# Attention block in float32: operand sums moved between GpSimd and VectorE, stores and loads reordered, fixed operand slots

## Chip, cores and metric

One core of one Trainium2 chip. The time is the device time of one execution in microseconds (us). All arithmetic is float32.

## The reference

x is 4 batches of 512 rows by 1024. The block computes `x + s * g`, with both branches fed by the layer-normed rows `xn`:

```
q = rmsnorm(xn @ Wq.T) * q_norm_w      32 heads of 128, k and v 8 heads (groups g of 4 query heads)
scores = q @ k.T / sqrt(128) + alibi bias, causal;  attn = softmax(scores)
s = concat_heads(attn @ v) @ Wo.T
g = silu(xn @ W.T + bias + lora(xn))   8 adapters of rank 16, weighted
```

## The kernel before, in words

Every large product is done as Strassen-Winograd: seven products of half-size blocks instead of eight, with block sums ahead of them and behind. The seven have the names `A11B11, A12B21, S2T2, S1T1, S3T3, A22T4, S4B22` (L36); S1 to S4 are sums of quadrants of the left operand, T1 to T4 of the right one.

**Front.** The rows are layer-normed, transposed, and the seven left operands of each half batch are written to the DRAM tile `xs`. The left half of the gate product (`f0`) is computed here, its result stored in the DRAM tile `pre`.

**Attention** runs over 32 *units*: a group g (8) and in it a batch b (4). I number them 0 to 31, n = 4 g + b. The order of SyncE (all loads: `sync_dma`), VectorE, ScalarE and TensorE is the order in the program (`in_order`, L69 to L94); GpSimd's is the scheduler's. The loop over units is L685 to L724:

- `fill` is a generator of the 14 projection products (q, k, v) of the *next* unit; each `steps(fill, 1)` issues one. Its left operands stream in from `xs` (`a<-xs`, up to 6 ahead, L433).
- *Lead phase*: eight such steps. Between them SyncE issues 16 `qkT<-flat` transfers of this unit (`turn_qk`, L478) and 16 `pt<-turned` transfers of the unit before (`spread`, L574), three pt per step. Both rearrange data across partitions.
- `attend` (L503): scores, the bias and row minimum on VectorE, exp on ScalarE, and `vector.transpose` of the probabilities into the one buffer `turned`. A new unit may write `turned` only when all 16 pt transfers of the last have read it. PSUM for scores has 3 buffers, `pr` has 6.
- `values` (L587) of the unit before runs late in `attend`: 10 products `ov<-pt,v`, copied by ScalarE to `oh`. Then GpSimd makes the left-operand sums S1 to S4 of the output product, four `tensor_tensor` on `oh` (L607 to L610), and stores all seven left operands in the DRAM tile `lo` of batch b (L611, 1792 KB).
- In odd units `out_sums` (L635) loads two rows of blocks of `wo` (1024 KB), makes the right-operand sums T1 to T4 on GpSimd (L641 to L644) and stores them in the DRAM tile `wt` (L645, 1024 KB).
- The weights of the next group are loaded in units with b = 0 and b = 2, and summed on GpSimd (`right_sums`, L198 to L201).

The last unit has the right half of the gate product (`f1`) for batch 0 as its fill; batch 1 goes beside its `spread`; then come its `values`, then batches 2 and 3 (L725 to L735).

**Output stage** (L738 on): s @ Wo.T as Strassen on two levels. 2 batch pairs times 7 outer products make 14 *items*, each of 7 inner products (`products`, L859) of 16 matmuls of 128x128x256. Inner operands: four quadrants left (`l`, from `lo`, 1 MB each) and right (`r`, from `wo` or `wt`, 1 MB each), four *head sums* (S, 128x2048, VectorE) and four *column sums* (T, 128x2048, GpSimd). `prepare` (L758) makes an item's operands while the item before is multiplied: a `yield` stands after each inner product. It takes tiles from two rings of 9 buffers. One head sum is issued at the fourth of its steps, the other three together at the sixth (L803 to L805), three column sums at the seventh (L807 to L809). Bank `u` takes the products 1, 3 and 5; VectorE saves it (`k`, L888) between these. In 8 of 14 items the finished quadrant is multiplied with the gate, `silu(pre + bias)`, added to x and stored (`gate`, `finish`, L835 to L855). The operands of the first item are loaded after the front pools are closed (L945).

Of the kernel before, what the change touches and what calls it, by code (L numbers as in the profile page):

```python
# [50 lines left out]
def kernel(  # L51
# [87 lines left out]


# [64 lines left out]
    with ExitStack() as front:  # L205
# [207 lines left out]
        with ExitStack() as mid:  # L413
            apool = mid.enter_context(tc.tile_pool(name="left", bufs=6))
            unit = mid.enter_context(tc.tile_pool(name="unit", bufs=2))
            work = mid.enter_context(tc.tile_pool(name="work", bufs=2))
            keep = mid.enter_context(tc.tile_pool(name="keep", bufs=1))
            ps_ov = mid.enter_context(tc.tile_pool(name="ps_ov", bufs=2, space=PSUM))
# [12 lines left out]
            loaded, later = {}, []  # L431
# [13 lines left out]
            def project_qkv(u, b, right, held):  # L445
                flat = unit.tile([P, 4, NT, G + 1, 32], F32, tag="flat", name=f"flat_{u}", bufs=1)
# [31 lines left out]
            def turn_qk(u, held):  # L478
                flat = held.pop("flat")
                qkT = unit.tile([P, 4, NT, G + 1, 32], F32, tag="qkT", name=f"qkT_{u}", bufs=1)  # L480
                for a in range(4):
                    for r in range(4):
                        sync_dma(
                            out=qkT[32 * a : 32 * a + 32, r].rearrange("p t h e -> p (t h e)"),
                            in_=flat[32 * r : 32 * r + 32, a].rearrange("p t h e -> p (t h e)"),
                        )
                        if (4 * a + r) % 5 == 4:
                            yield
                held["qkT"] = qkT

            def scale_k(u, held):
                qkT = held["qkT"]
                kT = unit.tile([P, NT, 4, 32], F32, tag="kT", name=f"kT_{u}", bufs=1)
                vector.tensor_scalar(
                    kT,
                    qkT[:, :, :, 0, :].rearrange("p r t e -> p t r e"),
                    w_sb,
                    None,
                    ALU.mult,
                )  # L500
                held["kT"] = kT
# [72 lines left out]
            def spread(u, held):  # L574
                pt = unit.tile([P, G, npairs, P], F32, tag="pt", name=f"pt_{u}", bufs=1)
                src = turned.rearrange("p m n t e -> p m (n t e)")
                for h in range(G):
                    for m in range(4):
# [4 lines left out]
                        if (4 * h + m) % 3 == 2:  # L583
                            yield
                held["pt"] = pt

            def values(u, g, b, held):  # L587
                pt, v = held["pt"], held["v"]
                oh = unit.tile([P, NP, 2, 2, P], F32, tag="oh", name=f"oh_{u}", bufs=1)
                for i in range(NT):  # L590
# [16 lines left out]
                nc.gpsimd.tensor_tensor(oh[:, S1T1], a21, a22, ALU.add)  # L607
                nc.gpsimd.tensor_tensor(oh[:, S3T3], a11, a21, ALU.subtract)
                nc.gpsimd.tensor_tensor(oh[:, S2T2], oh[:, S1T1], a11, ALU.subtract)
                nc.gpsimd.tensor_tensor(oh[:, S4B22], a12, oh[:, S2T2], ALU.subtract)  # L610
                nc.gpsimd.dma_start(  # L611
                    out=lo[b][:, g], in_=oh.rearrange("p i k m q -> p i (k m) q")
# [22 lines left out]
            def out_sums(g, k):  # L635
# [5 lines left out]
                nc.gpsimd.tensor_tensor(b11, b12, b11, ALU.subtract)  # L641
                nc.gpsimd.tensor_tensor(b12, b22, b12, ALU.subtract)
                nc.gpsimd.tensor_tensor(b22, b22, b11, ALU.subtract)
                nc.gpsimd.tensor_tensor(b21, b22, b21, ALU.subtract)  # L644
                nc.gpsimd.dma_start(  # L645
                    out=wt[k][:, :, :, g, :].rearrange("p i n c -> p (i n) c"),
                    in_=w.rearrange("p k n (m c) -> p (k n m) c", m=2),
# [8 lines left out]
            def last_gate(b):  # L656
                if b == 0:
                    rights["f1"] = weight_operands(raw.pop(HKV), 4, "f1")
                yield from project(
                    f"f1_{b}", b, 4, stream(f"f1_{b}", b), rights["f1"], store_gate(b, 1)  # L660
                )

            def bias_of(g):
                bias = unit.tile([P, SPAN], F32, tag="bias", name=f"bias_{g}", bufs=1)
# [20 lines left out]
            for n, (g, b) in enumerate(units):  # L685
# [3 lines left out]
                fill = start_project(*units[n + 1]) if n + 1 < len(units) else last_gate(0)  # L689
                done = 0  # L690
                for _ in turn_qk(u, held[g, b]):
                    steps(fill, 1)
                    done += 1
                rest = iter(())
                if before is not None:
                    for _ in spread(f"{before[0]}_{before[1]}", held[before]):
                        steps(fill, 1)
                        done += 1
                        if done == LEAD - 2:
                            scale_k(u, held[g, b])  # L700
                    rest = values(f"{before[0]}_{before[1]}", *before, held.pop(before))
                else:
                    steps(fill, LEAD - 2 - done)
                    scale_k(u, held[g, b])
# [5 lines left out]
                for k, _ in enumerate(attend(u, g, b, held[g, b], bias)):  # L710
                    steps(fill, (1, 1, 1, 1, 1, 2, 0, 0)[k])
# [14 lines left out]
            fill = last_gate(1)  # L726
            for _ in spread(u, held[before]):
                steps(fill, 1)
            for _ in fill:
                pass  # L730
            for _ in values(u, *before, held.pop(before)):
                pass
            for b in range(2, B):
                for _ in last_gate(b):
                    pass  # L735


    with ExitStack() as back:  # L738
# [3 lines left out]
        right = back.enter_context(tc.tile_pool(name="right", bufs=9))  # L742
        left = back.enter_context(tc.tile_pool(name="heads", bufs=9))
# [3 lines left out]
        sync_dma(out=bias_bc, in_=bf.to_broadcast([P, D]))  # L747

        QC = D // 4
        quads = (11, 12, 21, 22)  # L750
        part = lambda q: ((q // 10 - 1), (q % 10 - 1))
        wo_of = {A11B11: (0, 0), A12B21: (1, 0), S4B22: (1, 1)}
        wt_of = {S1T1: 0, S3T3: 1, A22T4: 2, S2T2: 3}

        for n in range(6):
            right.tile([P, HKV, QC], F32, tag="r", name=f"rest_{n}")

        def prepare(bp, i, ops):  # L758
            name = f"{bp}_{i}"

            def rt(n):
                return right.tile([P, HKV, QC], F32, tag="r", name=f"r{n}_{name}")

            def lt(n):
                return left.tile([P, 2, HKV, P], F32, tag="l", name=f"l{n}_{name}")

            def load_right(q):
                w = rt(q)
                k, n = part(q)
                if i in wo_of:  # L770
                    kh, nh = wo_of[i]
                    c0 = 512 * nh + QC * n
                    sync_dma(
                        out=w,
                        in_=wo[:, :, 2 * kh + k, c0 : c0 + QC].rearrange("g p c -> p g c"),
                    )
                else:
                    sync_dma(out=w, in_=wt[k][:, wt_of[i], n])
                return w

            def load_left(q):
                a = lt(q)
                m, k = part(q)
                for b in range(2):
                    sync_dma(out=a[:, b], in_=lo[2 * bp + b][:, :, i, 2 * k + m, :])
                return a

            b12, a21 = load_right(12), load_left(21)
            b11, a11 = load_right(11), load_left(11)
            b21, a12 = load_right(21), load_left(12)  # L790
            yield
            t2, s2 = rt(2), lt(2)
            yield
            t1, s1 = rt(1), lt(1)
            nc.gpsimd.tensor_tensor(t1, b12, b11, ALU.subtract)
            yield
            t3, s3 = rt(3), lt(3)
            vector.tensor_tensor(s3, a11, a21, ALU.subtract)
            yield
            t4, a22 = rt(4), load_left(22)  # L800
            yield
            b22, s4 = load_right(22), lt(4)
            vector.tensor_tensor(s1, a21, a22, ALU.add)  # L803
            vector.tensor_tensor(s2, s1, a11, ALU.subtract)
            vector.tensor_tensor(s4, a12, s2, ALU.subtract)  # L805
            yield
            nc.gpsimd.tensor_tensor(t2, b22, t1, ALU.subtract)  # L807
            nc.gpsimd.tensor_tensor(t3, b22, b12, ALU.subtract)
            nc.gpsimd.tensor_tensor(t4, t2, b21, ALU.subtract)  # L809
            ops.update(  # L810
                {
                    A11B11: (a11, b11),
                    A12B21: (a12, b21),
                    S2T2: (s2, t2),
                    S1T1: (s1, t1),
                    S3T3: (s3, t3),
                    A22T4: (a22, t4),
                    S4B22: (s4, b22),
                }
            )  # L820
# [38 lines left out]
        def products(bp, i, ops):  # L859
# [12 lines left out]
            def product(acc, p, start):  # L872
                a, w = ops[p]
# [69 lines left out]
        items = [(bp, i) for bp in range(2) for i in range(NP)]  # L943
        ops = {}
        for _ in prepare(*items[0], ops):  # L945
            pass
        for n, (bp, i) in enumerate(items):
            after = {}
            ahead = prepare(*items[n + 1], after) if n + 1 < len(items) else iter(())
            for _ in products(bp, i, ops):  # L950
                next(ahead, None)
            ops = after
# [40 lines left out]
```

## Time and profile before

| | |
|---|---|
| median of 3 runs (lowest, highest) | 2836.09 us (2822.3, 2838.67) |
| profiled execution: time, span | 2833.2 us, 2831.3 us |
| TensorE busy, VectorE, ScalarE, GpSimd | 93%, 52%, 28%, 35% of the span |
| granted TensorE clock, mean | 0.98 |
| front, until the first qkT transfer | 0 to 229 us |
| attention, 31 units with the next unit beside them | 229 to 1920 us |
| last unit and right gate half | 1920 to 2072 us |
| output stage | 2076 to 2831 us |

In the lines of the timeline the first two numbers are start and length in us, then engine, line, operation, `out<-in`, shape and how many were merged; `[3.0 <-X]` says that the engine stood idle 3.0 us before and that X ended it. `SPq` are DMA issues of SyncE: the length is that of the issue, not of the transfer. Line 92, 77 and 87 are the recording helpers for matmul, for VectorE and ScalarE, and for SyncE's transfers, so the tiles tell the instructions apart. A suffix `_p` is the q, k, v projection, `_f` the gate, `_o` the output stage.

### The profile page before, as it was taken

The numbers are of one execution on the slowest core, as the hardware profiler recorded it, in microseconds if no ns is written. First come the engines' busy times: TensorE is split into PE (matmuls) and PEld (weight loads), VectorE is DVE, ScalarE is ACT, GpSimd is POOL, SyncE is SP. The second block draws the span as 40 slices with busy tenths as digits, with TensorE's granted clock in tenths as the row PEclk, the third lists the DMA queues.
The fourth block names the chain that finished last, engine by engine and source line by source line (L and its number), as shares of the span: only waits on it lengthen the run. The fifth ranks groups of instructions, "written<-read, shape, count | busy, mean of one in ns | idle before, by whom it ended". The sixth has DMA issues, their size and how long they took to land.

```text
span 2831.3 us, 29439 instructions
## 1 busy us (share of the span) xinstructions
PE 2645.1 (93%) x9448; PEld 1777.3 (63%) x9448; DVE 1461.3 (52%) x3211; ACT 793.0 (28%) x2112; POOL 1002.3 (35%) x740
## 2 busy tenths in 40 slices
PE   6898999999999999999999999998869999999998
PEld 4664555555555555555555555556658887888877
DVE  5315455455545545645454555454035547755465
ACT  1113344334434434434343444344000000000000
POOL 5331232332332332242143143233133543535433
PEclk9999999999999999999999999999989999999999
DMA  5633776777678678678767876776786656675652
GB/s 220 248 130 112 210 215 178 213 206 220 194 208 238 176 216 218 192 205 212 207 172 222 208 209 189 218 217 182 227 248 197 209 163 197 199 213 191 200 180 73
DMA packets 344537, 561.43 MB, mean 198 GB/s; under 512 B 32320, under 2 KB 222784, under 8 KB 334784
## 3 DMA queue, kind: packets, MB, share of 16 engines
q1 hardware_dynamic: 328464, 450.48, 57.1%
q0 software_dynamic: 14080, 92.28, 8.8%
q10 hardware_dynamic: 1840, 16.78, 1.5%
q8 instruction: 77, 1.26, 0.2%
q14 instruction: 76, 0.62, 0.1%
HBM read 324.54 MB, written 109.05 MB: 153 GB/s over the span
## 4 chain that ended last, share of the span: by engine, by line
PE 61%; DMA 14%; SPq 9%; issue 6%; DVE 6%; POOL 3%; ACT 1%; ACTq 0%; POOLq 0%; DVEq 0%
PE c_p L92 15%; PE u_p L92 10%; SPq L87 9%; PE c_o L92 9%; PE ov L92 8%; PE u_o L92 8%; DMA pt<-turned 7%; PE sc L92 6%; DMA a<-xs 3%; PE c_f L92 3%; PE u_f L92 2%; DVE l L77 1%; DMA row<-in_x_dram 1%; DVE ms L77 1%; ACT pr L77 1%
## 5 line engine op out<-in xcount | busy, mean ns | idle before, releaser
L92 PE MATMUL c_o<-r,l 128*128 128x256 f32 x1792 | 393.6, 379 | 0.0
L92 PEld LDWEIGHTS c_o<-r,l 128*128 128x128 f32 x1792 | 340.5, 190 | 46.3
L92 PE MATMUL c_p<-t_q,a 128*128 128x384 f32 x1024 | 357.8, 493 | 9.7 <-DMA a<-xs 8.6
L92 PE MATMUL u_o<-r,l 128*128 128x256 f32 x1344 | 314.3, 394 | 56.2 <-DVE k L77 33.9
L77 DVE TENSOR_TENSOR c_p<-c_p,k_p 128x384 f32<-128x384 f32 x192 | 107.1, 558 | 484.3 <-ACT k_p L77 274.0
L92 PE MATMUL u_p<-t_q,a 128*128 128x384 f32 x1024 | 353.1, 488 | 3.2 <-DMA a<-xs 2.9
L77 ACT ACTIVATE pr<-sc,low 128x128 f32<-128x128 f32 (+12 forms) x512 | 248.5, 488 | 383.4 <-DVE low L77 219.4
L92 PE MATMUL c_p<-b,a 128*128 128x384 f32 x1024 | 351.7, 486 | 0.5 <-DMA a<-xs 0.5
L92 PE MATMUL sc<-kT,qkT 128*128 128x128 f32 (+12 forms) x1024 | 300.0, 410 | 46.3 <-ACT pr L77 46.1
L92 PEld LDWEIGHTS u_o<-r,l 128*128 128x128 f32 x1344 | 266.5, 199 | 98.4 <-issue 54.2
L92 PE MATMUL ov<-pt,v 128*128 128x512 f32 x640 | 291.4, 594 | 0.0
L92 PEld LDWEIGHTS sc<-kT,qkT 128*128 128x128 f32 x1024 | 178.6, 191 | 174.0 <-ACT pr L77 75.8
L92 PEld LDWEIGHTS c_p<-t_q,a 128*128 128x128 f32 x1024 | 195.3, 193 | 140.3 <-issue 11.1
L451 POOL COPY v<-c_p 128x128 f32<-128x128 f32 x128 | 37.8, 295 | 685.9 <-DVE c_p L77 685.9
L92 PEld LDWEIGHTS c_p<-b,a 128*128 128x128 f32 x1024 | 192.2, 190 | 128.9 <-PE sc L92 0.8
L77 DVE STREAM_TRANSPOSE turned<-pr 128x128 f32<-128x128 f32 (+6 forms) x800 | 214.3, 332 | 113.8 <-DMA a<-xs 35.3
L92 PEld LDWEIGHTS u_p<-t_q,a 128*128 128x128 f32 x1024 | 191.4, 190 | 128.0 <-DMA a<-xs 7.1
L77 DVE CUSTOM_DVE_ANT_0 sc<-sc,bias 128x128 f32<-128x128 f32 (+12 forms) x512 | 223.7, 466 | 59.3 <-PE sc L92 56.8
L77 ACT ACTIVATE pr<-pr,rden 128x128 f32<-128x128 f32 (+12 forms) x512 | 230.3, 522 | 83.6 <-DVE rden L77 83.3
L77 DVE TENSOR_TENSOR l<-l,l 128x2048 f32<-128x2048 f32 x56 | 211.0, 3768 | 35.9 <-DMA l<-lo 31.9
L92 PEld LDWEIGHTS ov<-pt,v 128*128 128x128 f32 x640 | 121.5, 191 | 145.4 <-issue 126.4
L462 POOL TENSOR_TENSOR inv<-ms,neg_half 128x5 f32<-128x5 f32 x128 | 149.9, 1181 | 176.4 <-DVE ms L77 176.4
(112 smaller groups left out, 2798.4 us busy)
## 6 DMA issues: line engine op xcount, KB each, us to landing
a<-xs SPq DMA_DIRECT2D x448, 256.0 KB, 5.3
pt<-turned SPq DMA_DIRECT2D x512, 160.0 KB, 5.1
lo<-oh POOLq DMA_DIRECT2D x32, 1792.0 KB, 8.2
l<-lo SPq DMA_DIRECT2D x112, 512.0 KB, 7.6
qkT<-flat SPq DMA_DIRECT2D x512, 80.0 KB, 2.6
r<-wt SPq DMA_DIRECT2D x32, 1024.0 KB, 6.7
r<-in_wo_dram SPq DMA_DIRECT2D x24, 1024.0 KB, 6.3
b<-in_wq_dram SPq DMA_DIRECT2D x32, 512.0 KB, 7.5
```

The lines of the kernel that those rows point to most:

```text
L77: ins = getattr(self.engine, op)(*args, **kw)
L87: ins = nc.sync.dma_start(**kw)
L92: ins = nc.tensor.matmul(*args, **kw)
L451: nc.gpsimd.tensor_copy(v[:, t, :], c[:, G + 1, :])
L462: nc.gpsimd.tensor_tensor(inv, ms, neg_half, ALU.pow)
```

## The change

1. `values` no longer sums on GpSimd. The four S sums on `oh` become VectorE instructions, put as closures into the list `spare`; the last also issues the `lo` store. `out_sums` does the same with T and the `wt` store. In the lead phase, `lead()` issues one product of `fill` and then pops one closure of `spare`, first in first out: eight per unit.
2. The last unit has the gate products of batches 0 and 1 as its fill, two per step of `attend`. Its `spread` is cut into 16 steps of one transfer, beside the 28 gate products of batches 2 and 3; its `values` come after all of them.
3. Tiles that end with the last `attend` (`flat`, `qkT`, `kT`, `bias`, `pr`, `sq`, `wo`) lie in pools at the right end of SBUF. They are closed early; a pool `first` with six operand slots takes their place, and four operands of the first item (right 11, left 11, right 21, left 12; 4 MB) are loaded among the gate products (`opening`).
4. In the output stage the rings are replaced by named slots (L0 to L4, R0 to R4, S0 to S3, T0 to T3), and the class `Item` says which quadrant of the next item goes into which slot. All eight loads of an item are issued at its first three steps; then one head sum (VectorE) and one column sum (GpSimd) at each of the last four. Number, size and engine of these sums stay.

```diff
+        def ahead(self):
+            self.left(21)
+            self.right(12)
+            self.left(22)
+            self.right(11)
+            yield
+            self.left(11)
+            self.right(22)
+            yield
+            self.left(12)
+            self.right(21)
+            yield
+            for n in (1, 2, 3, 4):
+                self.heads(n)
+                self.columns(n)
+                yield
...
+    def open_first():
+        now.right(11)
+        yield
+        for q, b in ((11, 0), (11, 1), (12, 0), (12, 1)):
+            now.left(q, (b,))
+            yield
+            if (q, b) == (11, 1):
+                now.right(21)
+                yield
...
+            unit = mid.enter_context(tc.tile_pool(name="unit", bufs=1))
             keep = mid.enter_context(tc.tile_pool(name="keep", bufs=1))
+            short = mid.enter_context(ExitStack())
+            brief = short.enter_context(tc.tile_pool(name="brief", bufs=1, side="right"))
+            work = short.enter_context(tc.tile_pool(name="work", bufs=2, side="right"))
...
-                nc.gpsimd.tensor_tensor(oh[:, S1T1], a21, a22, ALU.add)
-                nc.gpsimd.tensor_tensor(oh[:, S3T3], a11, a21, ALU.subtract)
-                nc.gpsimd.tensor_tensor(oh[:, S2T2], oh[:, S1T1], a11, ALU.subtract)
-                nc.gpsimd.tensor_tensor(oh[:, S4B22], a12, oh[:, S2T2], ALU.subtract)
-                nc.gpsimd.dma_start(
-                    out=lo[b][:, g], in_=oh.rearrange("p i k m q -> p i (k m) q")
+                def store():
+                    vector.tensor_tensor(s4, a12, s2, ALU.subtract)
+                    nc.gpsimd.dma_start(
+                        out=lo[b][:, g], in_=oh.rearrange("p i k m q -> p i (k m) q")
+                    )
+                spare.extend(
+                    (
+                        lambda: vector.tensor_tensor(s1, a21, a22, ALU.add),
+                        lambda: vector.tensor_tensor(a21, a11, a21, ALU.subtract),
+                        lambda: vector.tensor_tensor(s2, s1, a11, ALU.subtract),
+                        store,
+                    )
                 )
...
+                def lead():
+                    steps(fill, 1)
+                    if spare:
+                        spare.pop(0)()
                 for _ in turn_qk(u, held[g, b]):
-                    steps(fill, 1)
+                    lead()
...
             u = f"{before[0]}_{before[1]}"
-            fill = last_gate(1)
-            for _ in spread(u, held[before]):
-                steps(fill, 1)
+            fill = last_gates(2, 3)
+            short.close()
+            pools["first"] = back.enter_context(
+                tc.tile_pool(name="first", bufs=1, side="right")
+            )
+            turns = spread(u, held[before], 1)
+            for n in range(4 * NP):
+                lead()
+                next(turns, None)
+                if n >= 10 and n % 3 == 1:
+                    next(opening, None)
             for _ in fill:
                 pass
+            for _ in opening:
+                pass
             for _ in values(u, *before, held.pop(before)):
                 pass
-            for b in range(2, B):
-                for _ in last_gate(b):
-                    pass
+            for task in spare:
+                task()
...
-            t2, s2 = rt(2), lt(2)
-            yield
-            t1, s1 = rt(1), lt(1)
-            nc.gpsimd.tensor_tensor(t1, b12, b11, ALU.subtract)
-            yield
-            t3, s3 = rt(3), lt(3)
-            vector.tensor_tensor(s3, a11, a21, ALU.subtract)
-            yield
-            t4, a22 = rt(4), load_left(22)
-            yield
-            b22, s4 = load_right(22), lt(4)
-            vector.tensor_tensor(s1, a21, a22, ALU.add)
-            vector.tensor_tensor(s2, s1, a11, ALU.subtract)
-            vector.tensor_tensor(s4, a12, s2, ALU.subtract)
-            yield
-            nc.gpsimd.tensor_tensor(t2, b22, t1, ALU.subtract)
-            nc.gpsimd.tensor_tensor(t3, b22, b12, ALU.subtract)
-            nc.gpsimd.tensor_tensor(t4, t2, b21, ALU.subtract)
```

## The prediction

> **What bounds the kernel now.** I read, in this order: the page's busy slices, TensorE's waits, the timelines of TensorE, SyncE, VectorE and GpSimd at the places those waits named, and the DMA share by short windows. TensorE is busy 2645 of 2831 us, so what can be won is its idle time, and the slow matmuls after it. Its waits:
>
> ```profile
> PE sc L92 <- ACT pr L77: 46.1, 35, 3.9
> PE u_o L92 <- DVE k L77: 33.9, 6, 6.7
> PE u_o L92 <- DMA l<-lo: 17.7, 1, 17.7
> ...
> PE u_o L92 <- POOL r L807: 4.6, 1, 4.6
> ```
>
> Columns: total us, times, longest. Rows two to four are the output stage, row one is the attention.
>
> *Output stage, second row.* A product is 32 matmul records and follows the one before by 6.905 us. Six times it does not:
>
> ```profile
> 2354.33 7.07 PE L92 MATMUL c_o<-r,l 128*128 128x256 f32 x32
> 2368.13 8.64 PE L92 MATMUL u_o<-r,l 128*128 128x256 f32 x32 [6.73 <-DVE k L77]
> 2376.61 7.07 PE L92 MATMUL c_o<-r,l 128*128 128x256 f32 x32
> ```
>
> The third product of an item comes 6.9 us late and itself takes 1.6 longer: it accumulates into bank u, which VectorE has not yet read into k. VectorE was busy with the item's head sums:
>
> ```profile
> 2193.01 15.33 DVE L77 TENSOR_TENSOR l<-l,l 128x2048 f32<-128x2048 f32 x3
> ...
> 2223.91 2.29 DVE L77 TENSOR_TENSOR l<-l,l 128x2048 f32<-128x2048 f32 x1
> ```
>
> ```profile
> 2199.64 6.55 POOL L808 TENSOR_TENSOR r<-r,r 128x2048 f32<-128x2048 f32 x1
> 2206.16 6.55 POOL L809 TENSOR_TENSOR r<-r,r 128x2048 f32<-128x2048 f32 x1
> ```
>
> Alone a head sum takes 2.29 and a column sum 4.5. Together, three head sums take 15.33: each waits for a GpSimd sum to end, and GpSimd's grows by 2.05. A k-save (one operand in PSUM) takes 0.68 in the middle of a GpSimd sum and does not wait.
>
> *The way into the output stage*, rows three and four:
>
> ```profile
> 2070.50 1.89 PE L92 MATMUL c_f<-b,a_f 128*128 128x256 f32 x8
> 2090.04 9.44 PE L92 MATMUL u_o<-r,l 128*128 128x256 f32 x32 [17.66 <-DMA l<-lo]
> 2099.32 7.07 PE L92 MATMUL c_o<-r,l 128*128 128x256 f32 x32
> ...
> 2110.94 8.86 PE L92 MATMUL u_o<-r,l 128*128 128x256 f32 x32 [4.55 <-POOL r L807]
> ```
>
> *Attention.* The wait of row one comes once in most units. Follow unit 26 back: the PSUM of scores waits for ACT, ACT for a free pr, that for VectorE's `turned<-pr`, and that until all 16 pt transfers of the unit before have read `turned`. Unit 1, the only one before which no lo store is issued, is the comparison:
>
> ```profile
> 303.43 0.51 SPq L87 DMA_DIRECT2D pt<-turned  x1
> ...
> 1676.35 0.51 SPq L87 DMA_DIRECT2D pt<-turned  x1
> ```
>
> ```profile
> 310.30 0.89 DVE L77 STREAM_TRANSPOSE turned<-pr 128x128 f32<-128x128 f32 x4 [1.64 <-issue]
> ...
> 1684.30 0.89 DVE L77 STREAM_TRANSPOSE turned<-pr 128x128 f32<-128x128 f32 x4 [3.19 <-DMA a<-xs]
> ```
>
> ```profile
> 1656.10 0.62 POOL L611 DMA_DIRECT2D lo<-oh  x1 [0.30 <-POOL oh L610]
> ```
>
> I count from a unit's first qkT issue (277.23 and 1647.79). In unit 1 the last pt is issued at +26.2 and `turned` opens at +33.1; TensorE does not wait. In the others the lo store goes out at about +8.2, `turned` opens at a mean of +36.1, and TensorE waits about 1.1. So a lo store, before pt, costs 3.0. And the opening sets the unit: unit 12 opens at +34.7 and lasts 52.5, unit 24 opens at +38.5 and lasts 56.2. 1 us later is 1 us more, from about +35 on.
>
> DMA share (second last column), before the pt phase of unit 1, late in that of unit 26, and at the end of unit 25:
>
> ```profile
> 285.00:288.00 3.00, 3.00 (x11) 1.77 (x10) 0.00 (x0) 0.48 (x1) 0.00 (x0) 1.00 0.69 193
> ...
> 1672.00:1675.00 3.00, 3.00 (x13) 1.96 (x12) 1.29 (x3) 0.00 (x0) 0.00 (x0) 1.00 1.05 236
> 1645.00:1648.00 3.00, 3.00 (x8) 1.33 (x7) 2.93 (x5) 0.86 (x2) 0.00 (x0) 1.00 0.05 19
> ```
>
> **The change, part by part.** The sum is against the profiled execution, 2833.2 us (span 2831.3), 2.9 below the median of 2836.1.
>
> *Output stage: one head sum per product, columns beside it.* The counts stay (4 head, 4 column sums an item). Before, three head sums met three column sums in one product. I walk the gated case in the new order, from the end of product 3 (0; products end every 6.9), with each SBUF sum of VectorE put behind the GpSimd sum that runs then: head 1 ends at 8.8; three PSUM reads, then finish and gates around columns 3 and 4, bring head 2 to 28.2; head 3 to 34.7; finish and head 4 to 39.1; the next k to 39.8. It is needed at 41.4. The two S3T3 items add three sums of 0.69 and miss by about 0.5. Lost before: 33.9 waiting, 13.3 by which those six products ran over 6.905 (1.5 + 1.6 + 3.0 + 3.1 + 2.4 + 1.7), and 1.0 between the recorded waits and the late starts: 48. I take **-46**. Bounds: -48; and -20 if the late k comes back in half of the places.
>
> *First operands loaded among gate products, values last.* Lost now: 17.8 + 2.4 + 4.7 + 1.8 = 26.7. After, a11, b11, a12, b21 are there, values (8.6) come between, and product 1 starts at once. Product 3, due 22.4 after the last gate product (8.6 + 13.8), needs T2 = b22 - (b12 - b11). Those loads are queued on SP behind the gates (R2 lies where the gate weights were): 4 MB at the 300 GB/s of the windows after 2080 is 14, with the tail of the opening loads about 20; GpSimd's first column stands behind the last lo store, which waits for four VectorE sums after the values. So T2 at 27 to 30: a wait of 6 and 2.5 of slow clock, **-18** (bounds -26.7 and -10).
>
> *Gate products around the last unit.* They lose 28 now: 20.7 waiting for a_f or pr, the rest at lower clock. The lead phase of unit 31 keeps its loads and its wait (11 of 12). In the second phase pt goes one per product instead of three, but 4 MB of operands, wt and lo_2 come in: about 55 us of DMA work to the last a_f against 48 of products. **-5**, bounds -15 and +5.
>
> *Attention: sums from GpSimd to VectorE, four per unit and four more in every second.* On VectorE 128 + 64 sums of 0.69 (the row of gt<-sig,gt), 133 us of a VectorE that is a little over half busy there. They stand in the lead phase, where it waits for puts, so I charge nothing; if that cover failed, a put 0.69 late still meets a bank that is needed one product (2.58) later. GpSimd's 247 us off its queue gain nothing: TensorE never waits for it here. But the stores move with the sums. In odd units the four oh sums are done after the second product's put: the lo store goes from +8.2 to +10.2. In even units from 2 on the queue first holds the wo sums: the wt store, until now issued at +46 of the unit before where the DMA is idle, goes out at +10, and the lo store after the seventh product, at +22, in the middle of pt. Prices:
>
> ```profile
> q0 software_dynamic: 14080, 92.28, 8.8%
> ```
>
> That is 249 us for 92.28 MB, 2.7 us a MB: lo (1.84 MB) 4.95, wt (1.05) 2.8. Before pt a third of the DMA is free and takes some of it up (3.0 instead of 4.95); within pt none is. The trace has that case once: the lo store of 1982.2, 2.5 us into the pt of unit 31. That pt phase lasted 20.1 (1979.7 to 1999.8) against 14.5 in unit 1: 5.6 more. So even units open at 33.1 + 2.3 (wt, less 0.5 of free DMA) + 4.95 = 40.3 instead of 36.6 (mean of the 15; units 4 and 20, without a recorded opening, taken 1.0 ahead of TensorE's wait): 3.7 each, **+55** for 15. Their wait grows to 5; waits of 3.6 and 4.6 (1937.9, 2110.9) were followed by 1.6 and 1.8 of slow matmuls, part of which falls on score rows: 1.2 each, **+18**. Odd units: 2 us less of a third of free DMA, 0.6 each, **+10** for 16. Bounds: the lo store behind pt, costing nothing, with wt at 1.7 for lo's 3.0: -20 in all; or 5.6 and 1.7 in each even unit and 1.9 in each odd: +135.
>
> Two rules of the Trainium skill bear on this, and the sum does not need them. "DMA: Bandwidth & Descriptors" (Queues, rings and completion order) says that each DMA engine takes turns between its queues, packet by packet; by it the store, though from another queue, gets its turn amid pt, takes about 10 us, and pt pays all of its 4.95; the one row (5.6, landing 11.8 instead of 8.1) agrees, and by that row +55 would be +65. "TensorE: Matmul & The Clock Gate" (Part 1) halves the clock after an idle window of about 3.4 us; by it my 15 longer waits cost up to 1.7 each, an estimate, +26 for my +18, while the rows show 1.3 lost even after a wait of 1.9 (1957.1).
>
> Startup and last item keep their work: 0. Sum: -46 - 18 - 5 + 55 + 18 + 10 = +14, so 2847.
>
> **Rivals.**
> 1. *Stores cost attention nothing.* For it: they run on another queue, and odd units barely change. Against: the share of 1.0 throughout pt, and unit 31. It ends faster: 2833 - 69 - 10 = 2754 (-20 at best, 0 where wt costs what lo cost). It decides from the point where even units open before +37.
> 2. *VectorE is the new bound in the output stage.* For it: head sum and column are now issued in the same product, so every product can collide, and my walk leaves 1.6 of 6.9. Against: six collisions of three were worse. With -20 for -46 it is 2873, slower; it decides if k comes 2 us later than in the walk.
> 3. *The gate products starve.* About 10 MB of operands, pt, wt and lo share one DMA: if each of 28 products waits 1 us, +28 instead of -5: 2880.
> 4. *The transfers ahead change nothing*, because T2 is late anyway: product 3 would wait 20, and 18 of gain fall away: 2865.
>
> **How the numbers follow.** Likeliest, 0.60: the output stage wins about 70 and attention returns it, 2847, own range 2805 to 2885. Rival 1: 0.25. Rivals 2 to 4 together: 0.15, 2865 to 2905. 1% (28 us) is about what a measurement tells from no change. Faster 0.30 (rival 1 and the fast edge of the likeliest, 0.05), within 1% 0.43 (the likeliest's middle), slower 0.27 (0.14 of the likeliest, 0.13 of the rest). The range, 2760 to 2890, reaches to rival 1's centre and rival 2's.
>
> **What would show it.** Right: no wait of u_o for DVE k above 1; one wait of 3 to 9 at the third product of the output stage; lo stores at +22 in every second attention unit with `turned` opening near +40 and units of 57 to 61 us there, others near 54.5. Wrong: even units below 56 (then rival 1), k waits in the gated items, or long a_f waits after the last scores. Most likely to be wrong is the share of the DMA that the lo store takes from pt.

## The result, and the profile after

| | before | after |
|---|---|---|
| median of 4 runs, us | 2831.07 (2822.3 to 2838.67) | 2865.27 (2861.26 to 2874.79) |
| profiled execution: time, span | 2833.2, 2831.3 | 2861.26, 2859.5 |

The changed kernel takes 1.0127 times as long (95% interval 1.0083 to 1.0171): 34 us more by the medians, 28.2 between the two profiled spans, where +14 was forecast. By stage:

| stage, as cut in the two timelines | before | after | measured | forecast |
|---|---|---|---|---|
| start, until the first qkT issue | 229.3 | 230.3 | +1.1 | 0 |
| attention, first qkT issue of unit 0 to that of unit 31 | 1690.8 | 1755.8 | **+65.0** | +83 |
| unit 31 and gate products, without the way into the output | 152.3 | 147.2 | -5.1 | -5 |
| way into the output stage (time lost) | 26.7 | 17.9 | **-8.8** | -18 |
| output stage (time lost on 98 products of 6.905) | 48.1 | 24.4 | **-23.7** | -46 |
| end | 7.2 | 7.0 | -0.2 | 0 |

Every step that was forecast went its way, all but one (the gate products) with about half to four fifths of its size. TensorE's waits after (total us, times, longest):

```profile
PE sc L92 <- ACT pr L77: 58.2, 38, 3.9
PE u_p L92 <- DMA a<-xs: 39.3, 26, 3.1
PE c_o L92 <- DVE c L77: 16.2, 3, 6.2
PE u_o L92 <- issue: 14.7, 1, 14.7
```

The 33.9 us for `k` and the 17.7 us for the first operands are gone. Three waits have come in their place, and none of them was in the prediction in this form: attention waits for `a`, a left operand of the projection (this row was 7.1 us before); three output products wait for `c`; and one for what the profile calls "issue".

**Attention.** The stores went where the prediction put them (from GpSimd's timeline, unit 6, whose first qkT issue is at 559.1):

```profile
569.39 0.89 POOL L770 DMA_DIRECT2D wt<-wo  x1 [14.99 <-DVE wo L77]
...
581.73 0.55 POOL L728 DMA_DIRECT2D lo<-oh  x1 [1.10 <-ACT sq L77]
```

```profile
598.02 0.89 DVE L77 STREAM_TRANSPOSE turned<-pr 128x128 f32<-128x128 f32 x4 [5.59 <-DMA a<-xs]
```

That is wt at +10.3, lo at +22.6, and `turned` open at +38.9 (35.0 in the same unit before). Over the 15 even units the opening moved from 36.6 to 39.2 and the period from 55.8 to 58.5. But the odd units, to which the prediction gave +0.6 each, became 1.8 longer (units 3 to 29: 53.9 to 55.7), and very unevenly: those with b = 3 went from 53.9 to 57.3, those with b = 1 only from 53.9 to 54.1. In both groups the lo store goes out ahead of pt: at +9.6 in six of the seven units with b = 3, at +10.4 in those with b = 1. Unit 7 (b = 3) and unit 9 (b = 1) from +18 to +30; the last two columns are the share of the time that the DMA was busy and GB/s:

```profile
636.94:648.94 12.00, 9.98 (x36) 6.03 (x35) 6.10 (x18) 3.46 (x11) 2.66 (x3) 1.00 1.06 198
753.24:765.24 12.00, 12.00 (x46) 7.69 (x45) 6.88 (x24) 4.41 (x14) 2.66 (x3) 1.00 1.02 248
```

In the five units with b = 3 that opened after +39 this rate was 193 to 198 GB/s, in the nine other odd units 218 to 248.

**Output stage, the wait for c.** TensorE, VectorE and SyncE in the timeline of after, at the first of the three:

```profile
2427.80 7.07 PE L92 MATMUL c_o<-T,L 128*128 128x256 f32 x32
2441.06 10.11 PE L92 MATMUL c_o<-R,S 128*128 128x256 f32 x32 [6.20 <-DVE c L77]
```

```profile
2433.32 2.24 DVE L77 TENSOR_TENSOR gt<-gt,bias_bc 128x512 f32<-128x512 f32 x1 [18.45 <-DMA gt<-pre]
2436.32 0.69 DVE L77 TENSOR_TENSOR gt<-sig,gt 128x512 f32<-128x512 f32 x1 [0.76 <-ACT sig L77]
2436.93 2.29 DVE L77 TENSOR_TENSOR S<-L,L 128x2048 f32<-128x2048 f32 x1
2439.13 1.28 DVE L77 TENSOR_TENSOR k<-x,u_o 128x512 f32<-128x512 f32 x2
2440.33 0.68 DVE L77 TENSOR_TENSOR c<-k,c_o 128x512 f32<-128x512 f32 x1
```

```profile
2400.39 0.37 SPq L87 DMA_DIRECT2D xr<-in_x_dram  x1
2400.85 1.24 SPq L87 DMA_DIRECT2D L<-lo  x2
...
2422.97 2.73 SPq L87 DMA_DIRECT2D R<-in_wo_dram  x1
2425.74 1.72 SPq L87 DMA_DIRECT2D gt<-pre  x1
```

Read from the bottom up: SyncE issues all operands of the next item (8 L and 4 R transfers, 8 MB, from 2400.85 on) ahead of this item's second gate, so `gt` is issued at 2425.74 and is there at 2433.3. VectorE has stood still for 18.45 us at the bias sum of that gate, and k and c, which need no DMA, stand behind it. Product 7 accumulates into the bank that c reads. It happens in the three gated items after which an item comes whose R is read from `wo`; where R is read from `wt`, SyncE is through about 6 us sooner. The same three are also the only gated items, among those with a next item, that follow a gated one. In them the operand loads start late, behind this item's own first gate (its `xr` goes out at 2400.39): the first R is issued 7.1 to 9.3 us after the item's first product starts (2402.2 against 2392.93 here), and 0.1 to 0.2 after it in the four gated items that have a next item and no such wait. Which of the two is needed for the wait, no run parts.

**The way into the output stage.**

```profile
2134.00 7.17 PE L92 MATMUL u_o<-R,L 128*128 128x256 f32 x32 [0.68 <-ACT oh L77]
2141.01 7.07 PE L92 MATMUL c_o<-R,L 128*128 128x256 f32 x32
2162.79 9.29 PE L92 MATMUL u_o<-T,S 128*128 128x256 f32 x32 [14.71 <-issue]
```

Product 1 starts 0.7 after the value rows, as meant, and product 3 waits 14.7 (forecast 6). The chain of waits, in the window of this wait, says what it is made of (start, length, what):

```profile
2137.26 5.93 DMA lo<-oh
...
2143.52 0.39 SPq L87
...
2146.27 9.24 DMA R<-in_wo_dram
...
2155.64 4.81 POOL T L210
2160.45 2.34 issue
2162.79 9.29 PE u_o L92 x32
```

The R loads for T2 are not issued after the gate weights are done with, as the prediction had it (last gate product: 2124.7), but from the moment when the *last lo store has landed* (2143.2): 18.5 us later.

### The profile page after: what moved, and what is told of

Its sections match the earlier page's. It is cut to its first block, busy times and chain, and to the rows that moved or that the text cites. A ratio compares the mean times of both kernels' runs of the same rounds, so it can differ in the third digit from the quotient of the medians.

```text
span 2859.5 us, 29523 instructions
## 1 busy us (share of the span) xinstructions
PE 2652.3 (93%) x9448; PEld 1777.1 (62%) x9448; DVE 1529.1 (53%) x3403; ACT 793.5 (28%) x2112; POOL 751.8 (26%) x548
## 4 chain that ended last, share of the span: by engine, by line
PE 61%; DMA 17%; SPq 8%; DVE 6%; issue 4%; POOL 2%; ACT 1%; ACTq 0%; POOLq 0%; DVEq 0%
PE c_p L92 17%; PE u_p L92 10%; PE c_o L92 9%; SPq L87 8%; PE ov L92 8%; PE u_o L92 7%; DMA pt<-turned 6%; PE sc L92 6%; DMA a<-xs 5%; PE c_f L92 3%; PE u_f L92 2%; DMA R<-in_wo_dram 1%; DMA a_f<-xs 1%; POOL T L210 1%; DMA row<-in_x_dram 1%
## 5 line engine op out<-in xcount | busy, mean ns | idle before, releaser
L77 ACT ACTIVATE pr<-pr,rden 128x128 f32<-128x128 f32 (+12 forms) x512 | 230.3, 522 | 81.5 <-DVE rden L77 81.4
L568 POOL COPY v<-c_p 128x128 f32<-128x128 f32 x128 | 49.1, 384 | 755.8 <-DVE c_p L77 755.8
L92 PE MATMUL u_o<-T,S 128*128 128x256 f32 x896 | 200.3, 382 | 14.9 <-issue 14.7
L92 PEld LDWEIGHTS u_o<-T,S 128*128 128x128 f32 x896 | 171.5, 192 | 39.6 <-issue 16.0
L77 ACT COPY k_p<-u_p 128x384 f32<-128x384 f32 x192 | 91.5, 476 | 343.0 <-PE u_p L92 342.7
L92 PE MATMUL u_p<-b,a 128*128 128x384 f32 x512 | 177.8, 491 | 4.6 <-DMA a<-xs 4.6
L210 POOL TENSOR_TENSOR T<-R,R 128x2048 f32<-128x2048 f32 x28 | 136.9, 4888 | 112.6 <-PE u_o L92 74.7
```

The costliest lines, as they stand in the source:

```text
L77: ins = getattr(self.engine, op)(*args, **kw)
L92: ins = nc.tensor.matmul(*args, **kw)
L210: nc.gpsimd.tensor_tensor(d, a, b, ALU.subtract)
L568: nc.gpsimd.tensor_copy(v[:, t, :], c[:, G + 1, :])
```

## Experiments

Each ratio is against runs of the kernel before on the same chip.

### Is it the sums at all?

**both_back**: the changed kernel, the eight sums and the stores as before (shown for oh; wo alike).

```diff
-                spare.extend(
...
+                nc.gpsimd.tensor_tensor(s1, a21, a22, ALU.add)
+                nc.gpsimd.tensor_tensor(a21, a11, a21, ALU.subtract)
+                nc.gpsimd.tensor_tensor(s2, s1, a11, ALU.subtract)
+                nc.gpsimd.tensor_tensor(s4, a12, s2, ALU.subtract)
+                nc.gpsimd.dma_start(
```

> The changed kernel with the eight attention sums back on GpSimd, issued at once, so both stores stand where they stood before; all else stays changed. If the attention's loss of 65 us comes from the sums and stores (either their engine or their place), it goes: 2865 - 65 = 2800, even units near 55.8 and odd near 53.7 us, `turned` open near +36. If it comes from something else in the change (the two-sided pools, say), the time stays near 2865.

Measured: 2801.95 us, ratio 0.9871 (0.9849 to 0.9893). Even units 55.7, odd 53.8. All of the attention's loss lies in this one part of the change; the rest of the change wins 37 us.

### Which of the two stores?

**wt_back** makes the edit of both_back in `out_sums` alone, **lo_back** in `values` alone:

```diff
 wt_back, in out_sums:
-                spare.extend(
...
+                nc.gpsimd.tensor_tensor(b11, b12, b11, ALU.subtract)
...
 lo_back, in values:
-                spare.extend(
...
+                nc.gpsimd.tensor_tensor(s1, a21, a22, ALU.add)
```

> Only the wt sums and store go back to GpSimd at their old place; the oh sums stay on VectorE among the lead products, so lo goes out at +10 in every unit. By the place of the stores: odd units unchanged (55.4), even units lose wt's DMA work and have lo ahead of pt again: opening near 37, period near 56.2, so 15 x 2.3 = 35 less, 2830. If the engine is the cause, VectorE keeps two thirds of its sums and the time falls by a third of 65, to 2843.

Measured: 2849.04 us, ratio 1.0040 (1.0022 to 1.0059). Near the number, by other units than expected: even ones stayed at 58.1, odd ones at 56.2, though no wt store stands ahead of pt any more and lo goes out at +9.6 to +10.4 in all units. With the sums on VectorE and the store two us later, a unit takes over 2 more than in both_back, not 0.6.

> Only the oh sums and the lo store go back to GpSimd at once (+8); the wt sums stay on VectorE, the wt store goes out ahead of pt near +10 in even units. By the place of the stores: odd units back at 53.7 (-26 in all), even units open 1 to 1.9 later than in the kernel before for wt's 2.8 us of DMA work, so -12 to -25 there: 2814 to 2827. If the lo store within pt carries nearly all of the loss of the even units, the low end; if wt carries it, even units stay near 58.5 and the time is 2839.

Measured: 2870.21 us, ratio 1.0104 (1.0086 to 1.0121): missed. Odd units are back at 54.0, but even ones rose to 60.4: with lo at +8.6 and wt at +10.6 to +11.8 right behind it, both ahead of pt, they are worse off than with lo in the middle of pt. The two parts do not add up.

### Engine or place?

**gpsimd_late**: the closures of `spare` call GpSimd instead of VectorE.

```diff
-                        lambda: vector.tensor_tensor(s1, a21, a22, ALU.add),
+                        lambda: nc.gpsimd.tensor_tensor(s1, a21, a22, ALU.add),
```

> The changed kernel with the eight sums on GpSimd again, but still one after each product of the lead phase, so the stores keep their new, late places. If the place of the stores is the cause, the time stays at 2865 within 10, with even units near 58.5 and the lo store at +22 to +24. If the load on VectorE is the cause (its sums holding up puts and reads), it falls by most of 65, to about 2800 to 2810.

Measured: 2810.31 us, ratio 0.9906 (0.9876 to 0.9936). This run decides nothing: GpSimd's order is the scheduler's, not the program's, and the stores went back to +8.1 to +8.7. It is both_back again.

**late_store**: three of each four sums on GpSimd at once; the fourth, with the store, on VectorE at its late place (shown for oh; wo alike).

```diff
+                nc.gpsimd.tensor_tensor(s1, a21, a22, ALU.add)
+                nc.gpsimd.tensor_tensor(a21, a11, a21, ALU.subtract)
+                nc.gpsimd.tensor_tensor(s2, s1, a11, ALU.subtract)
...
+                spare.extend((lambda: None, lambda: None, lambda: None, store))
```

> The changed kernel, but the first three of each four attention sums go back to GpSimd, at once; only the fourth sum, with the store behind it, stays on VectorE at its late place. So VectorE has a quarter of the sums, and both stores go out where they do in the changed kernel (wt and odd lo near +10, even lo near +22). If the place of the stores is the cause, the attention's loss stays and the time is 2865 within 8. If VectorE's sums are the cause, three quarters of the loss go: 2802 + 16 = 2818.

Measured: 2870.20 us, ratio 1.0140 (1.0119 to 1.0161): the whole loss, with a quarter of VectorE's sums. Even units (wt at +8.8 to +9.8, lo at +21.7) 59.0, odd ones 55.1, their stores at +8.1 to +8.8, so earlier than was meant.

**vector_early**: wt as in wt_back; the four oh sums on VectorE right behind the first product.

```diff
+                def sums():
+                    vector.tensor_tensor(s1, a21, a22, ALU.add)
+                    vector.tensor_tensor(a21, a11, a21, ALU.subtract)
+                    vector.tensor_tensor(s2, s1, a11, ALU.subtract)
+                    store()
+                spare.append(sums)
```

> The wt part is as before; the four oh sums stay on VectorE, but all four stand right behind the first product of the lead phase, so that the lo store goes out near +5 instead of +10. All of VectorE's oh sums are there, only the place moves. If place is the cause, units are as in the kernel before (55.8 and 53.7) or shorter, and the time is 2802 or a little less, like the kernel with both sums back. If the engine is the cause, the time stays at that of the kernel with only wt back, 2849.

Measured: 2836.09 us, ratio 1.0013 (0.9996 to 1.0029), between the two. The place was missed too: the lo store went out at +8.7 to +9.7, not at +5, so this run does not part engine from place either.

**late_gpsimd**: the kernel before, with the last oh sum issued three times on GpSimd.

```diff
                 nc.gpsimd.tensor_tensor(oh[:, S4B22], a12, oh[:, S2T2], ALU.subtract)
+                nc.gpsimd.tensor_tensor(oh[:, S4B22], a12, oh[:, S2T2], ALU.subtract)
+                nc.gpsimd.tensor_tensor(oh[:, S4B22], a12, oh[:, S2T2], ALU.subtract)
```

> The kernel before, nothing of the change in it, but the last of GpSimd's four oh sums is issued three times (it writes the same values each time), 2.5 us of GpSimd work ahead of the lo store, which so goes out at +10.6 instead of +8.2. VectorE has nothing more to do. If the place of the lo store by itself lengthens the units, the time grows by 47 or more, as between the kernel with both sums back and the one with lo late on VectorE: 2880 to 2905, and the loss sits in units of the second and third batch row. If VectorE's sums are the cause, or my reading of the odd units is wrong, it stays within 10 of before.

Measured: 2835.90 us, ratio 1.0024 (0.9999 to 1.0050), the lo store at +10.8 to +11.9. So "later is worse" is wrong as it stands: taken alone this run spoke for the engine. (Its one trace, of an execution near the slow end of the ten, has the attention 18.9 us longer than before: 1709.7.)

**late_twin**: both_back, with the last oh sum issued twice.

```diff
                 nc.gpsimd.tensor_tensor(s4, a12, s2, ALU.subtract)
+                nc.gpsimd.tensor_tensor(s4, a12, s2, ALU.subtract)
```

> The kernel with both attention sums back on GpSimd, with one repeated oh sum (the same values again, 1.27 us of GpSimd), so that the lo store goes out at +9.4 to +10.0 instead of +8.1 to +8.8: about the place it has in the kernel with only wt back (+9.6 to +10.4), where the four sums ran on VectorE. Memory layout and wt are the same in both. If the place is what counts in the changed layout, the time is near that one: 2849, with units of the second and third batch row at 57 to 59 us. If it takes VectorE's sums as well, it stays near the kernel with both back, 2802 to 2808, as 2.6 us later cost the kernel before only 2.5.

Measured: 2870.20 us, ratio 1.0115 (1.0074 to 1.0156). One GpSimd sum of 1.27 us, with nothing more on VectorE, moves the lo store from +8.1 to +8.8 to +9.4 to +10.5 and costs 68 us against both_back. So in the changed layout the place is enough, and VectorE's sums are not needed for a loss of this size. Whether they add something of their own in the changed kernel or in vector_early, no run shows. Nor does a run show why late_gpsimd lost so little: its stores lie beyond +10.8 and its memory layout is that of before, and no run puts a store at +9.5 to +10.3 in that layout.

What happens to such a unit is seen within late_twin itself, in units 5 and 7 (first qkT issues at 499.1 and 612.9). GpSimd issues the lo store at +9.7 in the one and, its sums having begun 0.7 later, at +10.3 in the other, and here the later one does no harm:

```profile
508.73 0.62 POOL L731 DMA_DIRECT2D lo<-oh  x1 [0.30 <-POOL oh L730]
```

```profile
623.23 0.62 POOL L731 DMA_DIRECT2D lo<-oh  x1 [0.30 <-POOL oh L730]
```

Both tables run from +18 to +33 (last two columns as above); the store has landed, and pt and `a` are on the way:

```profile
517.10:520.10 3.00, 3.00 (x11) 1.76 (x10) 1.21 (x3) 0.22 (x1) 0.19 (x1) 1.00 1.05 206
520.10:523.10 3.00, 3.00 (x13) 1.99 (x12) 1.60 (x6) 2.24 (x7) 1.29 (x2) 1.00 1.07 200
523.10:526.10 3.00, 2.36 (x10) 1.37 (x9) 0.98 (x2) 0.19 (x2) 0.00 (x0) 1.00 1.01 167
526.10:529.10 3.00, 2.64 (x8) 1.63 (x9) 2.57 (x9) 0.81 (x4) 1.17 (x1) 1.00 1.12 220
529.10:532.10 3.00, 2.38 (x10) 1.52 (x9) 2.27 (x6) 2.42 (x9) 0.00 (x0) 1.00 1.00 197
```

```profile
630.90:633.90 3.00, 3.00 (x10) 1.71 (x9) 1.06 (x3) 0.00 (x0) 0.00 (x0) 1.00 1.02 250
633.90:636.90 3.00, 3.00 (x13) 1.97 (x12) 1.75 (x6) 1.84 (x3) 0.93 (x2) 1.00 1.07 246
636.90:639.90 3.00, 3.00 (x13) 1.97 (x12) 0.73 (x4) 0.81 (x4) 0.55 (x1) 1.00 1.00 249
639.90:642.90 3.00, 3.00 (x13) 2.00 (x12) 2.93 (x9) 1.28 (x5) 1.17 (x1) 1.00 1.07 251
642.90:645.90 3.00, 3.00 (x12) 1.94 (x11) 2.30 (x8) 2.05 (x9) 0.00 (x0) 1.00 1.02 230
```

The DMA is just as busy in both and moves 198 GB/s in the first against 245 in the second. The mix of packets is nearly the same, but each takes longer: from +18 to +30 one of pt's 5120 bytes 428 ns in the mean against 333, one of `a`'s 2048 bytes 174 against 136. `a` then comes late (the first column after the length is TensorE's busy time: 2.4 of 3 us), SyncE waits for its slots, the last pt comes late and `turned` opens at +39.4 against +35.8. Unit 5 lasts 57.2, unit 7 lasts 53.6.

```profile
538.44 0.89 DVE L77 STREAM_TRANSPOSE turned<-pr 128x128 f32<-128x128 f32 x4 [3.76 <-DMA a<-xs]
```

```profile
648.66 0.89 DVE L77 STREAM_TRANSPOSE turned<-pr 128x128 f32<-128x128 f32 x4 [1.76 <-DMA a<-xs]
```

Of the 29 units 2 to 30 of late_twin, 18 open at +38 or later, with 200 GB/s in the mean from +18 to +30; the other 11 have 231. In both_back it is one of 29.

### The wait for c

**gate_early**: gt and x rows of an item's second gate loaded right behind those of the first, ahead of the next item's operands.

```diff
             g11 = ready(11, gates(11))
+            x22 = gates(22)
...
-            g22 = gates(22)
+            g22 = ready(22, x22)
```

> The changed kernel with the gt and x rows of the second gate of an item loaded by SP ahead of the next item's operands, not behind them; the VectorE work on them stays where it is. If the three waits of product 7 for c (16.2 us and 7.4 of slow clock behind them) come from VectorE waiting 18 us for that gt, with k and c queued behind, they go: 2865 - 23 = 2842. If VectorE just has too much to do there, they stay: 2865.

Measured: 2858.98 us, ratio 1.0093 (1.0068 to 1.0118), 6 less than the changed kernel, which the intervals do not part. The three waits for c are gone, but two for k of 6.8 and 6.2 us have come: VectorE now waits 6.4 for the operands of a head sum, and 10.2 for the *third* gate, which SyncE still issues behind the operands.

**gates_four**: on both_back, three gates of an item loaded at its start (three buffers each for gt and xr).

```diff
+            loads = {q: gate(bp, i, q) for q in (11, 22, 21)} if last else {}
+            gates = lambda q: apply(bp, i, q, loads.get(q) or gate(bp, i, q)) if last else None
```

> Both attention sums back on GpSimd (2802), and in the output stage three of the four gates of an item loaded by SP at its start, ahead of the next item's operands (three buffers for gt and xr). If VectorE waiting for gt behind 8 MB of operands is the cause of the three waits for c, all three go, with none for k in their place: 2802 - 23 = 2779. If VectorE then waits for the operands of its head sums instead, k comes late in two of the three places and the gain is under 10.

Measured: 2786.02 us, ratio 0.9844 (0.9798 to 0.9890), 16 less than both_back by the medians (the intervals of the two ratios overlap). The traces show where: from the first output product to the end of the last it takes 706.9 us against 723.1. No wait for c is left, and this of k, in two places (neither forecast had that with so large a gain):

```profile
PE u_o L92 <- DVE k L77: 7.6, 2, 4.0
```

### The way into the output stage

**values_amid**: unit 31's value rows after the 22nd gate product instead of after the last.

```diff
                 if n >= 10 and n % 3 == 1:
                     next(opening, None)
+                if n == 21:
+                    for _ in values(u, *before, held.pop(before)):
+                        pass
```

> The changed kernel with unit 31's value rows after the 22nd gate product instead of behind all 28. If the third output product waits 14.7 because the R load for T2 has to wait until the last lo store has landed (its slot lies where oh was), the store now goes out about 10 us earlier against that product and the wait falls under 4: 2865 - 14 = 2851. If the load waits for the gate weights, or the DMA is the limit, the wait stays or grows by the 8.7 us that no longer cover it: 2865 to 2870.

Measured: 2864.70 us, ratio 1.0112 (1.0097 to 1.0127), no change. The wait fell to 11.5, not under 4. From its GpSimd and SyncE timelines:

```profile
2139.74 0.54 POOL L728 DMA_DIRECT2D lo<-oh  x1 [17.92 <-issue]
2141.96 1.07 POOL L386 DMA_DIRECT2D pre<-c_f  x2 [1.67 <-DVE c_f L77]
```

```profile
2147.98 0.39 SPq L87 DMA_DIRECT2D R<-in_wo_dram  x1
```

Here the chain of waits names `pre<-c_f`, which lands at 2147.65: now the R load waits for the last gate's store. So in both traces it waits for the store out of the closed pools that lands last. Which bytes of that slot each store still held is not traced.

**best**: gates_four and values_amid together.

> As the last, and with unit 31's value rows after the 22nd gate product, which gave 3.5 us in the transition of its trace: 2775 if the gates go as hoped.

Measured: 2780.89 us, ratio 0.9834 (0.9774 to 0.9893): 52 us under the kernel before by the medians of its own call, and 84 under the changed one's. Product 3 still waits 8.3 us.

## Why the prediction was right, and where it was not

*Output stage, -46: -23.7.* The mechanism held: with one head sum per product no k is late, and all 33.9 us of that wait are gone. What failed is the clause that the walk through the gated case rests on, "finish and gates around columns 3 and 4": it took the gates as ready. The change also moved eight operand loads past two gate loads on SyncE's queue, and the working never looked at SyncE. The new wait is not that of rival 2 (VectorE overloaded): VectorE stood idle for 18.45 of it, and gates_four won back 16 us with the same VectorE work, by loading gates earlier into three buffers instead of two (the order and the third buffer were not tried apart).

*First operands, -18: -8.8.* The step "(R2 lies where the gate weights were)" failed: the load waited 18.5 us more, until the last store from the closed pools had landed. Product 1 gained 19.3 of the 20.2 it was given, and product 3, with a wait of 14.7 where 6 was forecast, gave back 10.6 of it, where the forecast had 2.0: over halfway to rival 4, which had 20 for this wait.

*Gate products, -5: -5.1.* Right, by its sum; its parts were not measured one by one.

*Even units, +55 and +18: +40.* The store places were right to 1 us, and the opening came at +39.2 where 40.3 was forecast: 2.6 later than before, not 3.7. The period grew by 2.66, as much as the opening, so the second part, 1.2 of slow matmuls on top of it, does not show in the mean. But slow matmuls did come: the record of the granted clock has 0.50 for 3.4 us at a time in seven of the 15 even units, against two before, and of the 2.66 TensorE's busy time takes 0.57. Part of that falls ahead of the opening. The delay is split between a wait for `a` near +35 and one for pr near +40, of about 2 us each. Unit 6, with the clock (0.50) third from last in the second view:

```profile
593.54 2.85 PE L92 MATMUL u_p<-t_q,a 128*128 128x384 f32 x8 [1.64 <-DMA a<-xs]
596.22 0.65 PE L92 MATMUL sc<-kT,qkT 128*128 128x288 f32 x2
599.01 0.81 PE L92 MATMUL sc<-kT,qkT 128*128 128x320 f32 x2 [2.14 <-ACT pr L77]
599.66 4.44 PE L92 MATMUL c_p<-t_q,a 128*128 128x384 f32 x8
```

```profile
600.40:603.80 3.40, 3.40 (x7) 1.80 (x6) 2.46 (x12) 2.53 (x8) 2.82 (x2) 0.50 1.11 346
```

The eight products take 4.44 instead of 2.74. Where this falls behind the opening it lengthens the unit: units 3, 19 and 20 last 19.5 us beyond their opening, the other units of b = 0, 1 and 3 (from unit 4 on) 17.8 to 17.9. "TensorE: Matmul & The Clock Gate" of the Trainium skill (Part 1) halves the clock after an idle window of about 3.4 us. The idle stretch of 6.20 before 2441.06 agrees: a group of 10.11 instead of 7.07 follows. Unit 6 does not agree with it as a rule for single waits: no idle stretch there is longer than 2.14, and the clock is halved all the same.

*Odd units, +10: +25.* The step "2 us less of a third of free DMA, 0.6 each" failed. It counted bytes and free share. The trace shows a lower rate at full share in the units that open late (198 GB/s against 248 above), and late_twin that 1.3 us of place is enough for that. For the even units, with wt ahead of pt and lo amid it, that the place alone makes their loss is argued from these runs and not shown by one of its own. The same runs show that the 3.0 us which a lo store at +8.2 costs is no measure of what it costs at +9.5.

Rival 1 (stores cost attention nothing) fell with the result (even units open at +39.2, not before +37) and with both_back. Rival 3 fell with the -5.1 of the gate products. That the total, +28.2 between the traces, came as near to +14 as it did owes something to luck: the gains fell 31 us short and the losses of attention 18, and the two errors offset each other in part.

## What to carry to other kernels

When loads are moved up in a queue that runs in order, list what was in front of them before: here a 256 KB gate load fell behind 8 MB of operands, and the engine that waited for it held back work that needed no DMA at all. Before counting on the first load into newly opened memory, look for the last store out of what lay there, not the last matmul. And where a phase runs with the DMA at full share, price the move of a store by trying it at two or three places, alone and on its own engine: bytes and free share gave +73 where the even units lost 40, and +10 where the odd ones lost 25.

## What the runs showed of the hardware

The DMA's rate at full busy share is not one number. With pt (160 KB, SBUF to SBUF across partitions) and `a` (256 KB from DRAM) in flight, from +18 to +30, it was 238 to 250 GB/s in the four units of late_twin that opened by +36.5 and 190 to 199 in the ten that opened after +40. Over all the traces, counting units 2 to 30 with the lo store ahead of pt and no wt store there, an opening at +38 or later followed a store

| store issued at | opened at +38 or later | of units |
|---|---|---|
| +8.0 to +8.5 | 2 | 128 |
| +8.5 to +9.0 | 25 | 64 |
| +9.0 to +9.5 | 3 | 10 |
| +9.5 to +10.3 | 43 | 56 |
| +10.3 to +10.8 | 10 | 47 |
| +10.8 or later | 4 | 26 |

So it is not "the later, the worse": most late openings follow a store between +9.5 and +10.3, and beyond +10.3 they are rare again. All 56 units between +9.5 and +10.3 are in the changed layout, and 24 of the last 26 are in late_gpsimd, in the layout of before, so what belongs to the place and what to the layout is not parted. Why the rate falls, and stays low after the store has landed, is open; the order and spacing of pt were not varied.
